# Two batches' scores and attentions back to back, and the transposed weights in the buffer of the weights

## The chip, the core and the metric

The kernel runs on one core of one Trainium2 chip. The metric is device time in microseconds for one launch that computes the whole output. Before the change the median of three runs is 2391.39 us (2390.98 to 2392.63).

A core has a matrix engine (TensorE, PE in the profile, with its weight loads as PEld), VectorE (DVE), ScalarE (ACT), GpSimd (POOL) and SyncE (SP), which here issues nearly all DMAs. Each engine works through its own queue in program order and waits for the others by semaphores. TensorE writes to PSUM, 128 partitions of banks of 512 floats; all other tiles lie in SBUF.

## What is computed

Input `x` has 128 batches of 128 agents with 512 features, in float32, and `adj` one 128x128 adjacency matrix a batch. Two layers follow each other, each with a residual and a layer norm:

```
layer 0:  q, k, v = x Wq + bq, x Wk + bk, x Wv + bv         (8 heads of 64)
          attn    = softmax(where(adj > 0, q k^T / 8, -1e9))  over k, per head
          x1      = layernorm(x + relu(concat(attn v) Wo + bo))
layer 1:  Wh      = x1 W;  s_i = Wh a1;  s_j = Wh a2
          e       = where(adj > 0, leaky(s_i + s_j), -9e15);  att = softmax(e, over i)
          out     = layernorm(x1 + leaky(att Wh))
```

## The kernel before, in words

All products of a weight matrix are done by Strassen's scheme, seven products in place of eight. Q, K and V are made for a group of four batches (`group_product`, tiles `st_y`, `st_w`, `st_x`, L367): 21 pieces a group, 7 for each of Q, K and V, each of 8 TensorE instructions in the profile. The product with `Wo` (`LayerZero`) and with `W1` (`LayerOne`) are made for a pair of batches (`pair_product`, tiles `p_y`, `p_w`, `p_x`, L448): 7 pieces of 4 instructions each.

The softmax of layer 0 for one batch is the class `Softmax`. Its parts are

- `scores`: q k^T of the eight heads, two heads at a time, one on the upper and one on the lower 64 rows of TensorE's array, into two PSUM tiles `lg` (L519, 16 instructions);
- `add` (twice, L533) and `reduce` (L542) on VectorE: mask added while PSUM is read into `pa`, then the maximum of each head; `maxima` is all three;
- `exp` (L553) and `divide` (L567) on ScalarE, one instruction a head, with the sums of `exp` inverted on VectorE by `reciprocals` (L563);
- `store` (L574): `pa`, 512 KB, to DRAM; `fetch` (L580): back as `paz` in four DMAs, with blocks of 32 partitions rearranged; `transpose` (L584): 32x32 blocks turned on VectorE into `paT`. Together they make the transpose of each head's weights;
- `attend` (L597): O^T = V^T attn^T, two heads at a time on the two 64-column halves of the array, into one PSUM tile `p_oT` (16 instructions); `copy` (L611): to SBUF on ScalarE with the bias; `sum`: Strassen's sums of a pair on GpSimd.

Layer 1's attention of one batch is the class `Edge`, with one product `p_h` (L838) of two instructions.

The order of the work is written out by hand: the program switches the scheduler off, and each engine's queue holds its instructions in the order in which Python calls them. The main loop (L981) runs t from -3 to 123. In step t it interleaves a batch's softmax with `group()` (the next group piece), `pair()` (the next pair piece, `LayerZero` in odd steps and `LayerOne` in even ones), with the `Edge` of an earlier batch (`edge`, `fin`, `coming`) and with loads. Five group pieces fall on most steps (six on each fourth) and seven pair pieces. The last four batches and what is left over follow in a hand-written list, `PLAN` (L1242), in which `sl` is the softmax left over from the loop.

In the kernel before, step t does the whole softmax of batch t up to the fetch. Its transposition comes in the middle of step t + 1 (`last.transpose()`, L1097) and its attention at that step's end (`last.attend()`, L1146), just ahead of the next step's scores (L1017). At the end of a step the order on TensorE is therefore `p_h`, `p_oT` of the batch before, `lg` of the next batch, then a group piece.

`lg`, `p_oT`, `p_h`, `p_y`, `p_w` and `p_x` take turns in five PSUM banks (`ps_mm`, L98). `pa`, `paz` and `paT` have one buffer each, but in steps 0, 2 and 4 `pa` lies in another tile's place (`first_homes`).

## Time and profile before

| | us |
|---|---|
| median of three runs | 2391.39 |
| profiled execution, its own time | 2393.51 |
| span from first to last instruction | 2391.6 |
| TensorE busy | 2360.3 (99%) |
| VectorE busy | 1825.5 (76%) |
| ScalarE busy | 1515.4 (63%) |
| GpSimd busy | 814.6 (34%) |
| `lg` on TensorE, 128 blocks of 16 | 148.7 |
| `p_oT` on TensorE, 126 blocks of 16 (and two in other homes) | 137.9 |

The mean granted clock of TensorE is 0.998 of full speed. Between 200 and 2230 us TensorE is busy 2025.8 of 2030 us. The first 60 us hold 53.2 us of TensorE work and the last 161.6 us 143.5, so nearly all of its idle time lies at the two ends.

In a timeline a row is a run of instructions of one kind on one engine: start in us from the start of the span, length, engine, line, operation, output<-inputs, shapes and the number of instructions, and in brackets the idle time ahead of it with what ended it. TensorE's instructions overlap, so that a row's length runs into the next row: what a block costs is the distance from its start to the next start. For DMAs a row's length is the time of issuing; the landing is told separately.

### The profile page before, as it was taken

What the parts mean: (1) busy time and instruction counts of PE and PEld (TensorE: products, weight loads), DVE (VectorE), ACT (ScalarE), POOL (GpSimd) and SP (SyncE); (2) the same over time, 40 slices, a digit from 0 to 9 for tenths busy, and PEclk for the clock granted to TensorE, in tenths of its full rate; (3) what the DMA queues carried; (4) which work ended last, traced back from release to release, by engine and by line L of the source; (5) the groups of instructions that cost most, each with busy time, mean ns of one, the idle gap of its engine ahead of it and who ended that gap; (6) DMA issues with size and microseconds to landing.
All of it is one profiled execution on the core that took longest, in us unless ns stands there. A gap on an engine that the chain in (4) does not pass through costs nothing.

```text
span 2391.6 us, 44137 instructions
## 1 busy us (share of the span) xinstructions
PE 2360.3 (99%) x13362; PEld 1976.1 (83%) x13362; DVE 1825.5 (76%) x3718; ACT 1515.4 (63%) x5459; POOL 814.6 (34%) x1191
## 2 busy tenths in 40 slices
PE   8999999999999999999999999999999999999997
PEld 7888888888888888888888888888888888888875
DVE  5668777787787777877877877778777777787778
ACT  3656666666666666666666666666656666666675
POOL 1333334332343333333333433333323333333335
PEclk9999999999999999999999999999999999999999
DMA  7655555555555555555555555455555554545543
GB/s 204 183 176 157 158 178 156 175 156 161 170 159 168 179 153 169 164 163 180 156 159 178 161 166 166 155 174 164 160 182 159 155 181 148 185 157 161 166 154 115
DMA packets 435565, 395.31 MB, mean 165 GB/s; under 512 B 108280, under 2 KB 339328, under 8 KB 435328
## 3 DMA queue, kind: packets, MB, share of 16 engines
q1 hardware_dynamic: 435008, 392.23, 53.2%
q8 instruction: 107, 1.75, 0.3%
q14 instruction: 130, 1.06, 0.1%
q10 hardware_dynamic: 320, 0.26, 0.0%
HBM read 248.58 MB, written 143.72 MB: 164 GB/s over the span
## 4 chain that ended last, share of the span: by engine, by line
PE 84%; DVE 4%; DMA 4%; ACT 4%; SPq 2%; issue 2%; POOL 1%; DVEq 0%; POOLq 0%; ACTq 0%
PE st_y L367 24%; PE p_y L448 16%; PE st_w L367 12%; PE p_w L448 8%; PE st_x L367 6%; PE lg L519 5%; PE p_oT L597 5%; PE p_h L838 4%; PE p_x L448 4%; ACT pa L567 1%; DMA x_dram<-x 1%; ACT pa L553 1%; SPq L241 1%; DVE st L641 1%; DMA e_dram<-e 1%
## 5 line engine op out<-in xcount | busy, mean ns | idle before, releaser
L553 ACT ACTIVATE pa<-pa,nmax 128x128 f32<-128x128 f32 x1008 | 392.6, 394 | 8.4 <-DVE nmax L542 8.0
L647 POOL TENSOR_SCALAR ve<-mv 128x1 f32<-128x1 f32 x256 | 70.0, 273 | 840.2 <-DVE mv L643 834.8
L567 ACT ACTIVATE pa<-pa,rs 128x128 f32<-128x128 f32 x1008 | 334.1, 395 | 5.4 <-DVE rs L563 5.3
L276 POOL TENSOR_TENSOR oS<-oT 128x256 f32<-128x256 f32 x63 | 45.8, 728 | 639.2 <-ACT oT L611 639.2
L533 DVE TENSOR_TENSOR pa<-lg,mf 128x512 f32<-128x512 f32 x252 | 161.9, 684 | 95.2 <-PE lg L519 94.2
L459 ACT COPY pr_t<-p_y 128x257 f32<-128x257 f32 (+1 forms) x375 | 137.6, 367 | 131.8 <-PE p_y L448 127.7
L344 ACT COPY st_t<-st_y 128x512 f32<-128x512 f32 x192 | 110.5, 576 | 145.7 <-PE st_y L367 144.3
L553 ACT ACTIVATION_READ_ACCUMULATOR pa<-pa,nmax 128x1 f32 x1008 | 192.6, 191 | 0.0
L597 PEld LDWEIGHTS p_oT<-paT,v 128*64 128x64 f32 x2016 | 107.5, 136 | 93.2 <-PE st_y L367 44.0
L649 POOL TENSOR_TENSOR rstd<-ve,mhalf 128x1 f32<-128x1 f32 x256 | 177.0, 691 | 21.3
L611 ACT ACTIVATE oT<-p_oT,b_cols 128x128 f32<-128x128 f32 x504 | 144.2, 369 | 56.8 <-PE p_oT L597 55.8
L348 ACT ACTIVATE st_t<-st_y,b_cols 128x256 f32<-128x256 f32 x192 | 80.6, 471 | 155.3 <-PE st_y L367 155.3
L584 DVE STREAM_TRANSPOSE paT<-paz 128x1024 f32<-128x1024 f32 x126 | 156.9, 1245 | 8.2 <-DMA paz<-pa_dram 7.8
L542 DVE TENSOR_REDUCE nmax<-pa 128x8 f32<-128x1024 f32 x126 | 153.7, 1220 | 4.4
L519 PE MATMUL lg<-kT,qT 64*128 64x128 f32 x2048 | 148.7, 285 | 0.0
L519 PEld LDWEIGHTS lg<-kT,qT 64*128 64x128 f32 x2048 | 124.2, 187 | 22.9 <-issue 22.6
L597 PE MATMUL p_oT<-paT,v 128*64 128x128 f32 x2016 | 137.9, 279 | 1.5 <-DVE paT L584 1.0
L448 PE MATMUL p_y<-wo,oT 128*128 128x256 f32 x504 | 129.7, 380 | 1.9 <-ACT pr_t L459 1.7
L769 DVE TENSOR_TENSOR wh<-p_w,pr_t 128x257 f32<-128x257 f32 x122 | 51.9, 425 | 104.2 <-PE p_w L448 64.1
L448 PE MATMUL p_y<-w,x1T 128*128 128x257 f32 x496 | 128.3, 381 | 2.7 <-ACT wk L459 2.5
L448 PE MATMUL p_y<-wo,oS 128*128 128x256 f32 x504 | 129.6, 379 | 1.1 <-ACT pr_t L459 1.0
L448 PE MATMUL p_y<-w,x1S 128*128 128x257 f32 x496 | 128.1, 380 | 0.2 <-ACT wk L459 0.2
(201 smaller groups left out, 6024.2 us busy)
## 6 DMA issues: line engine op xcount, KB each, us to landing
pa_dram<-pa SPq DMA_DIRECT2D x126, 512.0 KB, 3.2
paz<-pa_dram SPq DMA_DIRECT2D x504, 128.0 KB, 2.8
wv_n<-wv SPq DMA_DIRECT2D x224, 256.0 KB, 2.8
x<-in_x_dram SPq DMA_DIRECT2D x128, 256.0 KB, 3.0
x_dram<-x SPq DMA_DIRECT2D x128, 256.0 KB, 2.6
xz<-x_dram SPq DMA_DIRECT2D x512, 64.0 KB, 2.0
xz<-in_x_dram SPq DMA_DIRECT2D x496, 64.0 KB, 2.3
out_dram<-z SPq DMA_DIRECT2D x120, 256.0 KB, 2.5
```

The costliest lines, as they stand in the source:

```text
L367: nc.tensor.matmul(p[:, m, :], lhs, rhs, start=start and m == 0 and kc == 0, stop=True, skip_group_check=True,)
L448: nc.tensor.matmul(p[:, :width], xs()[n][:, kc, :], w[:, PLACE[n], kc, :], start=start and kc == 0, stop=True, skip_group_check=True,)
L459: nc.scalar.copy(t[:, :width], p[:, :width])
L519: nc.tensor.matmul(self.lg[r][:, c, :], q[rows, c, cols], k[rows, c, cols], start=c == 0, stop=True, skip_group_check=True,)
L533: nc.vector.tensor_add(by_head[:, r * NC : (r + 1) * NC], self.lg[r].rearrange("p c (b k) -> p c b k", b=4), mf.unsqueeze(1).to_broadcast( ...
L542: nc.vector.tensor_reduce(self.nmax, by_head, AX.XY, ALU.max, negate=True)
L553: nc.scalar.activation(self.pa[:, :, h, :], self.pa[:, :, h, :], AF.Exp, bias=self.nmax[:, h : h + 1], accum_out=self.sums[:, h : h + 1],)
L567: nc.scalar.activation(self.pa[:, :, h, :], self.pa[:, :, h, :], AF.Copy, scale=self.rs[:, h : h + 1])
L584: nc.vector.transpose(self.paT.rearrange("p h (a i) -> p a h i", i=32), self.paz.rearrange("p a (h k) -> p a h k", k=32),)
L597: nc.tensor.matmul(self.oT[r * HD : (r + 1) * HD, c, :], v[:, h * HD : (h + 1) * HD], self.paT[:, r * NC + c, :], start=c == 0, stop=True, ...
L611: nc.scalar.activation(OT[pair][:, c, h * P : (h + 1) * P], self.oT[:, c, :], AF.Identity, bias=b_cols[:, 1, c : c + 1],)
L649: nc.gpsimd.tensor_tensor(self.r, ve, mhalf, ALU.pow)
```

## The change

The loop now handles two batches in two steps. In an even step t it makes the scores of batch t (`first`) and of batch t + 1 (`sm`) one behind the other, does the whole softmax of `first` up to the fetch, and of `sm` the adds, the reduction and the first four exponentials (at the end of the step). In the odd step it does the other four exponentials of `sm`, its divisions, its store and its fetch; it transposes `first` in the middle of the step and `sm` near the end; and then both attentions follow each other, then both copies, and the sums of the pair. The next even step begins with two scores again. So at the end of an odd step TensorE has `p_h`, `p_oT`, `p_oT`, `lg` x2 batches, and at the end of an even step `p_h` and then a group piece.

`transpose` writes into `pa` itself, which the store has emptied, viewed as [partition, head, query]; the tile `paT` is gone and `pa` has two buffers. Masks are loaded, cast and scaled two steps ahead instead of one. In `PLAN` the jobs of `sl` and `m1` go, since the loop now ends with all its batches attended. Setup tiles that borrowed the places of `pa`, `paz` and `paT` borrow the two of `pa`.

The diff, cut to its core (an odd step after the first few has the parts under `else`):

```diff
@@ class Softmax
         def tile(self, name, shape):
             home = self.homes and self.homes.get(name)
-            return home(shape) if home else work.tile(shape, F32, name=name)
+            bufs = 2 if name == "pa" else 1
+            return home(shape) if home else work.tile(shape, F32, name=name, bufs=bufs)
...
         def transpose(self):
-            self.paT = self.tile("paT", [P, H, P])
+            flat = self.pa.rearrange("p b h k -> p (b h k)")
+            self.paT = flat.rearrange("p (h q) -> p h q", h=H)
             nc.vector.transpose(
...
@@ main loop
-        if on(t + 1):
-            load_mask(t + 1)
+        if on(t + 2):
+            load_mask(t + 2)
...
-        last, sm = sm, Softmax(t, first_homes if t in (0, 2, 4) else None) if on(t) else none
-        sm.scores()
+        if t % 2 == 0:
+            first, sm = (Softmax(t), Softmax(t + 1)) if on(t) else (none, none)
+            first.scores()
+            sm.scores()
         coming.turn_blocks()
...
         else:
-            sm.maxima()
+            if t % 2 == 0:
+                first.maxima()
             group()
+            if t % 2 == 0:
+                sm.add(0)
+                sm.add(1)
...
             pair()
-            sm.exp(0, 1, 2, 3)
+            if t % 2 == 0:
+                first.exp(0, 1, 2, 3)
+            else:
+                sm.exp(4, 5)
             edge.exp()
             pair()
-            sm.exp(4, 5)
-            last.transpose()
+            if t % 2 == 0:
+                first.exp(4, 5)
+                sm.reduce()
+            else:
+                sm.exp(6, 7)
+                first.transpose()
             group()
-            sm.reciprocals(0)
+            (first if t % 2 == 0 else sm).reciprocals(0)
             pair()
-            sm.exp(6)
+            if t % 2 == 0:
+                first.exp(6)
+            else:
+                sm.reciprocals(1)
             fin.apply()
             fin.store()
-            sm.exp(7)
+            if t % 2 == 0:
+                first.exp(7)
+            else:
+                sm.divide(0, 1)
             edge.divide()
             pair()
-            sm.reciprocals(1)
-            sm.divide(0, 1, 2, 3)
+            if t % 2 == 0:
+                first.reciprocals(1)
+                first.divide(0, 1, 2, 3)
+            else:
+                sm.divide(2, 3, 4, 5)
             coming = Edge(t - 6) if on(t - 6) and t + 1 < END else none
             coming.sender()
             coming.store_sender()
...
             group()
-            sm.divide(4, 5)
+            if t % 2 == 0:
+                first.divide(4, 5)
+            else:
+                sm.divide(6, 7)
             pair()
-            sm.divide(6, 7)
-            if on(t + 1):
-                mask_float(t + 1)
+            if t % 2 == 0:
+                first.divide(6, 7)
+            if on(t + 2):
+                mask_float(t + 2)
             group()
-        sm.store()
+        (first if t % 2 == 0 else sm).store()
...
-        sm.fetch()
+        (first if t % 2 == 0 else sm).fetch()
...
+        if t % 2 == 0:
+            sm.exp(0, 1)
         pair(2)
+        if t % 2 == 0:
+            sm.exp(2, 3)
         if t % 2 == 0 and on(t - 6):
             turn_x1(t)
         if t not in (0, 4):
             group(21 if t % GROUP == 0 else 1)
+        if t % 2 == 1:
+            sm.transpose()
         fin = edge
         fin.product()
         fin.copy()
-
-        last.attend()
-        last.copy()
-        if t % 2 == 0:
-            last.sum(0, 1, 2, 3)
+        if t % 2 == 1:
+            first.attend()
+            sm.attend()
+            first.copy()
+            sm.copy()
+            sm.sum(0, 1, 2, 3)
```

Steps 0 to 4 have the same moves in their own branches, and `PLAN` loses the entries that begin with `sl.` and `m1.`.

More of the change, by code (lines that the diff above doesn't have):

```diff
@@ L175, in load_wv @@
         tiles = [big.tile([P, 2, 2, HALF], F32, name="wv_t", tag="v", bufs=3) for _ in range(3)]
-        tiles.append(work.tile([P, 2, 2, HALF], F32, name="wv_t", tag="paT"))
+        tiles.append(work.tile([P, 2, 2, HALF], F32, name="wv_t", tag="pa", bufs=2))
         t = [tiles[n // 2][:, n % 2] for n in range(7)]
@@ L897 @@
     chores = []
-    sm = fin = edge = coming = none
+    first = sm = fin = edge = coming = none
     def x_turns(t):
@@ L903, in x_turns @@
         return [b for b in [(), (t + 7, t + 8), (t + 8,), (t + 8,)][t % GROUP] if on(b)]
-    x_rows = [work.tile([P, 2, D], F32, name="x_rows", tag=tag) for tag in ("pa", "paz")]
+    x_rows = [work.tile([P, 2, D], F32, name="x_rows", tag="pa", bufs=2) for _ in range(2)]
     for b in range(2):
@@ L978 @@
     END = B - GROUP
-    first_homes = {"pa": lambda shape: work.tile(shape, F32, name="pa", tag="x1T")}
     for t in range(-3, END):
@@ L1025 @@
             group(2)
-        if t < 3:
-            sm.maxima()
+        if t < 3 and t % 2 == 0:
+            first.maxima()
+            sm.add(0)
+            sm.add(1)
             group(2)
@@ L1032 @@
                 sum_x(1)()
-            sm.exp(0, 1, 2, 3)
+            first.exp(0, 1, 2, 3)
             group()
+            first.reciprocals(0)
+            first.exp(4, 5, 6, 7)
+            first.reciprocals(1)
+            sm.reduce()
+            first.divide(0, 1, 2, 3)
+            group()
+            first.divide(4, 5, 6, 7)
+            mask_float(t + 2)
+        elif t < 3:
+            group(2)
+            if on(t - 2):
+                load_residual(t - 2)
+            sm.exp(4, 5)
+            group()
+            sm.exp(6, 7)
             sm.reciprocals(0)
-            sm.exp(4, 5, 6, 7)
+            sm.reciprocals(1)
             if t == 1:
                 group()
-            sm.reciprocals(1)
             sm.divide(0, 1, 2, 3)
-            last.transpose()
+            first.transpose()
             group()
@@ L1045 @@
                 group()
-            if on(t + 1):
-                mask_float(t + 1)
+            if on(t + 2):
+                mask_float(t + 2)
         elif t == 4:
             layer = later.pop()
-            sm.maxima()
+            first.maxima()
             group()
             layer.apply(0)
+            sm.add(0)
+            sm.add(1)
             load_residual(2)
@@ L1056 @@
                 sum_x(2)()
-            sm.exp(0, 1)
+            first.exp(0, 1)
             group()
-            sm.exp(2, 3, 4, 5)
-            last.transpose()
+            first.exp(2, 3, 4, 5)
+            sm.reduce()
             group()
@@ L1066 @@
             w1_chores(3)
-            sm.exp(6, 7)
+            first.exp(6, 7)
             group()
-            sm.reciprocals(0)
-            sm.reciprocals(1)
-            sm.divide(0, 1, 2, 3, 4, 5, 6, 7)
-            mask_float(5)
-        else:
-            sm.maxima()
+            first.reciprocals(0)
+            first.reciprocals(1)
+            first.divide(0, 1, 2, 3, 4, 5, 6, 7)
+            mask_float(6)
+        else:
+            if t % 2 == 0:
+                first.maxima()
             group()
+            if t % 2 == 0:
+                sm.add(0)
+                sm.add(1)
             if t == 3:
@@ L1092 @@
             pair()
-            sm.exp(0, 1, 2, 3)
+            if t % 2 == 0:
+                first.exp(0, 1, 2, 3)
+            else:
+                sm.exp(4, 5)
             edge.exp()
             pair()
-            sm.exp(4, 5)
-            last.transpose()
+            if t % 2 == 0:
+                first.exp(4, 5)
+                sm.reduce()
+            else:
+                sm.exp(6, 7)
+                first.transpose()
             group()
-            sm.reciprocals(0)
+            (first if t % 2 == 0 else sm).reciprocals(0)
             pair()
-            sm.exp(6)
+            if t % 2 == 0:
+                first.exp(6)
+            else:
+                sm.reciprocals(1)
             fin.apply()
             fin.store()
-            sm.exp(7)
+            if t % 2 == 0:
+                first.exp(7)
+            else:
+                sm.divide(0, 1)
             edge.divide()
             pair()
-            sm.reciprocals(1)
-            sm.divide(0, 1, 2, 3)
+            if t % 2 == 0:
+                first.reciprocals(1)
+                first.divide(0, 1, 2, 3)
+            else:
+                sm.divide(2, 3, 4, 5)
             coming = Edge(t - 6) if on(t - 6) and t + 1 < END else none
@@ L1117 @@
             group()
-            sm.divide(4, 5)
+            if t % 2 == 0:
+                first.divide(4, 5)
+            else:
+                sm.divide(6, 7)
             pair()
-            sm.divide(6, 7)
-            if on(t + 1):
-                mask_float(t + 1)
+            if t % 2 == 0:
+                first.divide(6, 7)
+            if on(t + 2):
+                mask_float(t + 2)
             group()
-        sm.store()
+        (first if t % 2 == 0 else sm).store()
         if 0 <= t < 3:
@@ L1134 @@
             load_x(b)
-        if on(t + 1):
-            mask(t + 1)
+        if on(t + 2):
+            mask(t + 2)
+        if t % 2 == 0:
+            sm.exp(0, 1)
         pair(2)
+        if t % 2 == 0:
+            sm.exp(2, 3)
         if t % 2 == 0 and on(t - 6):
@@ L1210 @@
         {"oT": spare("kT", 3)},
-        {"pa": spare("xT", 2), "paz": spare("xS", 2), "paT": spare("qT", 4)},
+        {"pa": spare("xT", 2), "paz": spare("xS", 2)},
         {},
-        {"pa": spare("xT", 2), "paz": spare("xS", 2), "paT": spare("qT", 4)},
+        {"pa": spare("xT", 2), "paz": spare("xS", 2)},
     ]
     fin.on_scalar = True
-    jobs = {"sl": sm, "el": fin, "v": Pieces(v_pieces)}
+    jobs = {"el": fin, "v": Pieces(v_pieces)}
     jobs["v"].fetch = fetch_v
@@ L1242 @@
     PLAN = """
-        el.residual v.p6 x0.x m2.adj m1.adj al.apply.0 x1.x e0.sender sl.transpose s0.scores
-        al.store.0 v.t2 al.fetch.1 v.p5 el.stats m2.cast s0.add.0 m1.cast el.rstd m3.adj s0.add.1
-        s1.scores al.fetch.0 s0.reduce el.apply b0.p1 m2.mask s0.exp.4.5 el.store m1.mask
-        s2.scores s1.add.0 v.fetch s0.exp.6.7 v.fetch s1.add.1 b0.p2 s0.exp.2.3 s1.reduce
-        sl.attend s0.exp.0.1 al.transpose.0 v.p2 s1.exp.6.7 al.transpose.1 s1.exp.2.3
-        s0.reciprocals.0 al.sum.0 s0.reciprocals.1 s0.divide.0.1 v.p7 al.sum.1 v.c11 v.fetch
-        s0.divide.6.7 al.sum.2 s0.divide.2.3 al.sum.3 b1.p1 s0.divide.4.5 v.t3 s0.store b0.t0
-        v.p4 v.c22 s1.exp.0.1 b0.c11 s1.exp.4.5 s1.reciprocals.0 v.p3 s1.divide.0.1 s2.add.0
-        s0.fetch s1.divide.2.3 s2.add.1 v.c21 s2.reduce b0.p6 e1.sender m3.cast b1.p5 sl.copy
-        m3.mask v.c12 s1.reciprocals.1 s2.exp.0.1 b1.p2 sl.sum.0 s0.transpose b0.t2 sl.sum.1
-        s1.divide.4.5 b0.p7 sl.sum.2 s1.divide.6.7 sl.sum.3 s2.exp.6.7 s1.store s2.exp.2.3 b0.t3
+        el.residual v.p6 x0.x m2.adj al.apply.0 x1.x e0.sender s0.scores al.store.0 v.t2
+        al.fetch.1 v.p5 el.stats m2.cast s0.add.0 el.rstd m3.adj s0.add.1 s1.scores al.fetch.0
+        s0.reduce el.apply b0.p1 m2.mask s0.exp.4.5 el.store s2.scores s1.add.0 v.fetch
+        s0.exp.6.7 v.fetch s1.add.1 b0.p2 s0.exp.2.3 s1.reduce s0.exp.0.1 al.transpose.0 v.p2
+        s1.exp.6.7 al.transpose.1 s1.exp.2.3 s0.reciprocals.0 al.sum.0 s0.reciprocals.1
+        s0.divide.0.1 v.p7 al.sum.1 v.c11 v.fetch s0.divide.6.7 al.sum.2 s0.divide.2.3 al.sum.3
+        b1.p1 s0.divide.4.5 v.t3 s0.store b0.t0 v.p4 v.c22 s1.exp.0.1 b0.c11 s1.exp.4.5
+        s1.reciprocals.0 v.p3 s1.divide.0.1 s2.add.0 s0.fetch s1.divide.2.3 s2.add.1 v.c21
+        s2.reduce b0.p6 e1.sender m3.cast b1.p5 m3.mask v.c12 s1.reciprocals.1 s2.exp.0.1 b1.p2
+        s0.transpose b0.t2 s1.divide.4.5 b0.p7 s1.divide.6.7 s2.exp.6.7 s1.store s2.exp.2.3 b0.t3
         s2.reciprocals.0 s2.exp.4.5 b0.p4 s2.divide.0.1 s1.fetch s2.reciprocals.1 b0.c21
```

## Prediction

> **What bounds the kernel now.** First the page's busy line, its chain, and the waits of TensorE's queue, longest first:

> ```profile
> PE 2360.3 (99%) x13362; PEld 1976.1 (83%) x13362; DVE 1825.5 (76%) x3718; ACT 1515.4 (63%) x5459; POOL 814.6 (34%) x1191
> PE 84%; DVE 4%; DMA 4%; ACT 4%; SPq 2%; issue 2%; POOL 1%; DVEq 0%; POOLq 0%; ACTq 0%
> PE p_h L838 <- DVE wk L833: 5.0, 5, 2.6
> PE p_y L448 <- ACT pr_t L459: 3.4, 7, 0.7
> ```

> TensorE is busy 99% of the span, and its longest sum of waits is 5.0 us. Only two things can move the time by a per cent: fewer TensorE microseconds, or a wait put into a queue that has none. The timeline of TensorE through one border between steps (start, length, operation) shows the first:

> ```profile
> 1003.03 1.02 PE L838 MATMUL p_h<-wh,att 128*128 128x512 f32 x2
> 1003.98 1.09 PE L597 MATMUL p_oT<-paT,v 128*64 128x128 f32 x16
> 1005.00 1.16 PE L519 MATMUL lg<-kT,qT 64*128 64x128 f32 x16
> 1006.10 1.99 PE L367 MATMUL st_y<-xT,wk 128*128 128x256 f32 x8
> 1007.93 1.03 PE L448 MATMUL p_y<-w,x1T 128*128 128x257 f32 x4
> ...
> 1009.66 1.89 PE L367 MATMUL st_y<-xT,wq 128*128 128x256 f32 x8
> 1011.39 1.03 PE L448 MATMUL p_y<-w,x1S 128*128 128x257 f32 x4
> ```

> Start to start, a Strassen product of eight instructions takes 1.73 us in ordinary running (1009.66 to 1011.39) but 1.83 behind the scores. p_h takes 0.95 here against 0.86 in the chain. p_oT (64 columns) takes 1.02 and the scores (64 rows) 1.10. What these two cost without their borders is read from two windows that cut a block in the middle:

> ```profile
> 1003.98 0.44 PE L597 MATMUL p_oT<-paT,v 128*64 128x128 f32 x4
> 1040.74 0.94 PE L519 MATMUL lg<-kT,qT 64*128 64x128 f32 x12
> ```

> p_oT: the twelve instructions after the first four take 1.09 - 0.44 = 0.65, so 0.108 per two and 0.87 for sixteen. Scores: the last four take 1.16 - 0.94 = 0.22, so 0.11 per two and 0.89 for sixteen.

> The second thing is how soon a batch's weights can be back on chip. One odd step, TensorE, ScalarE and SyncE:

> ```profile
> 1032.72 1.03 PE L448 MATMUL p_y<-wo,oS 128*128 128x256 f32 x4
> 1033.35 0.57 ACT L344 COPY st_t<-st_y 128x512 f32<-128x512 f32 x1
> 1033.82 0.69 ACT L567 ACTIVATE pa<-pa,rs 128x128 f32<-128x128 f32 x2
> 1034.67 0.70 ACT L567 ACTIVATE pa<-pa,rs 128x128 f32<-128x128 f32 x2
> 1035.39 0.32 SPq L574 DMA_DIRECT2D pa_dram<-pa  x1
> 1038.16 2.52 SPq L580 DMA_DIRECT2D paz<-pa_dram  x4
> 1038.76 1.02 PE L838 MATMUL p_h<-wh,att 128*128 128x512 f32 x2
> ```

> The last division ends at 1035.37, the store goes out at once, the fetch follows 2.77 us later when it has landed, and its four issues take 2.52. p_h, with attention right behind it, starts at 1038.76. Today that attention is of the batch before, so the trip has a whole step, 17.9 us, of cover.

> **The change, part by part.**

> *Fewer borders.* For each pair of batches one border of each kind goes: p_oT 1.02 - 0.87 = 0.15, scores 1.10 - 0.89 = 0.21, the product behind 0.10, p_h in the even step 0.09. That is 0.55 us a pair, all on TensorE, which is the path. The loop has 62 pairs: -34 us. The order of TensorE's instructions in the changed kernel shows 16 `p_oT` and 16 `lg` back to back, so the change does take place.

> *A round trip inside one step.* The second batch of a pair (`sm`) is now divided, stored, fetched, transposed and attended all in the odd step. Its last divisions stand on ScalarE behind the copy of that step's third group product, which waits for TensorE; so the trip cannot start early however idle ScalarE is. Ahead of that copy ScalarE has four exponentials less (1.55, from 1027.14 to 1028.69 for four) and two divisions more (0.6), some 0.95 less, so it reaches the copy before TensorE is done and waits for it. Two forms of odd step:

> (t % 4 = 3) Product done 1032.72; hand-over 0.20 (1007.93 to the copy at 1008.13); copy 0.47; two divisions 0.69: 1034.08, against 1035.37 before. Trip: issue to fetch 2.77 here and 2.65 a pair later (1072.67 to 1075.32), say 2.7; three issues ahead of the last, 1.3 to 1.9, say 1.6; landing of the last 2.8 (median of its DMA row); with hand-overs 0.2, 7.3. Landed 1041.4. The 128x1024 transposition takes 1.25 and the hand-over 0.1: 1042.7. TensorE comes to the second p_oT at 1038.76 + 0.95 + 0.92 (0.87 and a third of its border) = 1040.63. **Stall 2.1 us.**

> (t % 4 = 1) Product done 1070.18; hand-over 0.20; two half copies 0.73; divisions 0.69: 1071.8. Plus 7.3 and 1.35: 1080.45. TensorE: p_h at 1076.22, plus 1.87: 1078.09. **Stall 2.35 us.**

> Mean 2.25 a pair. Steps t = 3 to 123 are 61 pairs: +137 us. Nothing makes it shrink from pair to pair: the trip hangs on a TensorE product 7.9 us ahead of the attention, whenever that comes.

> Bounds of the trip: fastest landings and shortest issues of its rows (2.6 + 3 x 0.30 + 2.3 + 0.05) give 5.85, a stall of 0.8; the latest landing of any odd step in this trace gives 9.5, a stall of 4.45. I take 7.3 because both steps shown lie within 0.5 of it.

> [...]

> *Who is behind the new wait.* On VectorE the transposition waits for the landing; behind it stand `e_turned` (0.3), the x1 apply (0.55) and the next adds. They would be ready at 1042.6 + 0.85 = 1043.5, and the next scores are complete only at 1042.7 + 1.02 + 0.89 + 0.2 = 1044.8, so nothing more is late. On SyncE the fetch waits for the store as before, with the same loads behind it. On ScalarE the copies of p_oT start later with TensorE.

> *Moved work at no price.* Four exponentials (1.55) go to the end of the even step, where ScalarE idles 1.34 and 2.22 us (before L767 and L344). The even step gains two adds and a reduction on VectorE (1.29 + 1.22) and loses a transposition (1.25); it idled 0.66, 0.68, 1.84 and 2.21 there. Mask loads and casts come one step earlier, same number. The second scores need the PSUM bank of the first p_oT of the pair; ScalarE empties it in 1.14 after it ends, and TensorE comes 1.02 + 0.89 later. If that cover were gone it would cost 1.2 a pair; it isn't, and the stall widens it. The missing `paT` tile costs nothing: its place is `pa`, whose exponentials were stored before.

> *Start and end.* At t = 1 the last division ends near 61.2 in both (it follows a copy that waits for TensorE), store 62.68, four weight loads, last fetch issue 67.3, landed 70.1, transposed 71.5; TensorE is ready near 63.0: 8.5, less the 0.77 that it waits there now. +8 us. In the tail the jobs of `sl` leave the plan and one p_oT moves ahead of it: under 1 us either way, taken as 0.

> **Sum.** 2391.6 (span; its execution took 2393.5, the median run 2391.4, so span and median are one number here) - 34 + 137 + 8 = 2502.6. I say **2503 us**, 4.7% slower.

> **The rivals.**

> *Hidden trip: faster.* If the weights were back before TensorE asks, only -34 stays: 2358. It takes a trip of at most 5.2 us in the first form (from 1034.08 to 1040.63, less 1.35) and 4.95 in the second; the pair breaks even where the stall is 0.55, at a mean trip of 5.6. For it: the attention is the last thing in the step. Against: the fastest landings on the rows make 5.85. Chance 4%; level 1%.

> *Half hidden.* A trip of 5.85 to 6.3, the queues being calmer when TensorE runs 5% slower: stalls of 0.8 to 1.25, 2414 to 2442. For it: the DMA share is 0.54, not full. Against: the median landings, 3.2 and 2.8, lie only 0.6 and 0.5 above the fastest, so there is little queueing to lose. 8%.

> *Later still.* A trip over 8.3, or a second wait beside it (the first batch's transposition in the odd step also has only some 9 us from its divisions, and delays the second's divisions when late): over 2564, up to 2391.6 - 34 + 8 + 61 x 4.45 = 2637. 9%. A stall can also cost TensorE's clock: the granted clock stands at 1.00 in the first 60 us in spite of an idle of 1.8 us there.

> [...]

> *Forecast*, a trip of 6.3 to 8.3: stalls 1.25 to 3.25, 2442 to 2564. 78%.

> **How the numbers follow.** The time is that of the forecast. Its own range leaves 22% outside; I widen it by a few us on each side to 2438 and 2570. Faster by over 0.2% (4.8 us, about what a measurement can tell) 4%, within it 1%, slower 95%.

> **What would show it.** Right: TensorE's waits led by p_oT for VectorE's transposition, some 62 times, 2 to 2.5 us each and near 140 in total, between the two attentions; blocks of 32 `p_oT` and 32 `lg`; VectorE waiting for `paz`; PE's busy time down by about 34; the loop's pair of steps at some 37.5 us instead of 35.8. Wrong: p_oT waiting for nothing (hidden trip), or `lg` waiting for ScalarE's copies (banks). The step I trust least is the 7.3 us.

## The result, and the profile after

The changed kernel takes **2647.15 us** (median of four runs, 2639.35 to 2649.59) against 2391.33 (2390.98 to 2392.63) for the kernel before: 1.106 times as long, 95% interval 1.104 to 1.109. The forecast of 2503 had the sign and missed the size: the range ended at 2570.

The profiled execution after has a span of 2647.7 us; before it was 2391.6, so 256.1 us have to be found. First the page of the changed kernel, its busy line and the shares of its chain:

```profile
PE 2440.0 (92%) x13362; PEld 2069.0 (78%) x13362; DVE 1810.6 (68%) x3718; ACT 1515.2 (57%) x5459; POOL 796.9 (30%) x1191
PE 59%; DMA 15%; DVE 10%; ACT 7%; SPq 5%; issue 3%; POOL 1%; DVEq 0%; POOLq 0%; ACTq 0%
```

Two things are to be read here. TensorE's share fell from 99% to 92%, and in the chain DMA, VectorE, ScalarE and SyncE's queue (SPq) have 15, 10, 7 and 5% where they had 4, 4, 4 and 2: there is a wait now. But TensorE is also busy for 79.7 us longer, with the same 13362 instructions. A wait doesn't do that. Something made the instructions themselves longer.

The wait is the longest of TensorE's list of waits (us in total, times, longest):

```profile
PE p_oT L600 <- DVE pa L587: 176.9, 62, 7.1
```

The longer instructions are found in the groups by line and tile (count, then busy us and mean ns of one, then idle us before them):

```profile
L520 PE MATMUL lg<-kT,qT 64*128 64x128 f32 x2048 | 204.9, 377 | 0.0
L600 PE MATMUL p_oT<-pa,v 128*64 128x128 f32 x2016 | 160.2, 309 | 177.3 <-DVE pa L587 176.9 <-DVE rt L835 0.4
```

Before, the scores took 148.7 us in all and p_oT 137.9, in twice as many blocks. Fewer borders should have made both shorter. TensorE's timeline through one border of each form of odd step shows what happened. First t % 4 = 3:

```profile
1081.07 1.09 PE L600 MATMUL p_oT<-pa,v 128*64 128x128 f32 x16
1085.55 1.09 PE L600 MATMUL p_oT<-pa,v 128*64 128x128 f32 x16 [3.38 <-DVE pa L587]
1086.57 3.69 PE L520 MATMUL lg<-kT,qT 64*128 64x128 f32 x32
...
1123.22 1.09 PE L600 MATMUL p_oT<-pa,v 128*64 128x128 f32 x16
1126.49 1.09 PE L600 MATMUL p_oT<-pa,v 128*64 128x128 f32 x16 [2.18 <-DVE pa L587]
1127.51 3.69 PE L520 MATMUL lg<-kT,qT 64*128 64x128 f32 x32
```

The last three lines are the next odd step, t % 4 = 1. The two attentions stand together and the scores are one block of 32, as forecast; between the attentions is the stall, 3.38 and 2.18 us. The new thing is the length of the scores behind it: 3.69 us for 32 instructions, where 16 had taken 1.16 before. The trace's clock records give the reason: in 58 stretches, nearly all 3.413 or 6.827 us long and 238.8 us together, the clock was granted at half, nearly always from within 1.6 us of the end of such a stall. The mean clock of the run is 0.955. (The kernel before has one such stretch, of 13.0 us, at its very end.)

VectorE's timeline in the same two steps completes the picture. In the first the transposition waits for the data:

```profile
1081.57 0.52 DVE L665 TENSOR_SCALAR x<-x,mv,rstd 128x512 f32<-128x512 f32 x1
1084.24 1.25 DVE L587 STREAM_TRANSPOSE pa<-paz 128x1024 f32<-128x1024 f32 x1 [2.16 <-DMA paz<-pa_dram]
...
1124.17 0.51 DVE L665 TENSOR_SCALAR x<-x,mv,rstd 128x512 f32<-128x512 f32 x1
1124.60 0.68 DVE L385 TENSOR_TENSOR qT<-st_w,st_t 128x512 f32<-128x512 f32 x1
1125.20 1.23 DVE L587 STREAM_TRANSPOSE pa<-paz 128x1024 f32<-128x1024 f32 x1
```

In the second (last three lines) it waits for nothing: VectorE comes to it straight from a Strassen sum, the data having landed. So there the stall is not the trip's but the order of VectorE's own queue, in which the last group's sums and normalization stand ahead of the transposition.

The balance: +177 for the stall, some -33 for the borders (below), +107 for scores and p_oT at half clock (204.9 and 160.2 here, less 132.1 and 125.8, which is what the same blocks take in the last version below, which has no stalls). That makes 251 of 256 us.

### The profile page after: what moved, and what is told of

The parts are those of the page before. It is cut to its first block, busy times and chain, and to the rows that moved or that the text cites. A ratio compares the mean times of both kernels' runs of the same rounds, so it can differ in the third digit from the quotient of the medians.

```text
span 2647.7 us, 44071 instructions
## 1 busy us (share of the span) xinstructions
PE 2440.0 (92%) x13362; PEld 2069.0 (78%) x13362; DVE 1810.6 (68%) x3718; ACT 1515.2 (57%) x5459; POOL 796.9 (30%) x1191
## 4 chain that ended last, share of the span: by engine, by line
PE 59%; DMA 15%; DVE 10%; ACT 7%; SPq 5%; issue 3%; POOL 1%; DVEq 0%; POOLq 0%; ACTq 0%
PE st_y L367 16%; PE st_w L367 10%; PE p_y L448 10%; PE lg L520 7%; DMA pa_dram<-pa 7%; DMA paz<-pa_dram 6%; PE p_w L448 5%; DVE pa L587 4%; ACT pa L568 4%; PE st_x L367 4%; SPq L581 4%; PE p_oT L600 3%; PE p_x L448 3%; PE p_h L841 2%; DMA xz<-in_x_dram 1%
## 5 line engine op out<-in xcount | busy, mean ns | idle before, releaser
L568 ACT ACTIVATE pa<-pa,rs 128x128 f32<-128x128 f32 x1008 | 327.2, 393 | 26.5 <-DVE rs L564 26.2
L600 PE MATMUL p_oT<-pa,v 128*64 128x128 f32 x2016 | 160.2, 309 | 177.3 <-DVE pa L587 176.9
L600 PEld LDWEIGHTS p_oT<-pa,v 128*64 128x64 f32 x2016 | 124.4, 152 | 238.5 <-DVE pa L587 191.8
L534 DVE TENSOR_TENSOR pa<-lg,mf 128x512 f32<-128x512 f32 x252 | 161.7, 683 | 170.2 <-PE lg L520 170.2
L459 ACT COPY pr_t<-p_y 128x257 f32<-128x257 f32 (+1 forms) x375 | 138.1, 368 | 203.3 <-PE p_y L448 201.2
L344 ACT COPY st_t<-st_y 128x512 f32<-128x512 f32 x192 | 110.3, 574 | 192.8 <-PE st_y L367 192.5
L587 DVE STREAM_TRANSPOSE pa<-paz 128x1024 f32<-128x1024 f32 x126 | 156.7, 1244 | 80.3 <-DMA paz<-pa_dram 79.3
L520 PE MATMUL lg<-kT,qT 64*128 64x128 f32 x2048 | 204.9, 377 | 0.0
L520 PEld LDWEIGHTS lg<-kT,qT 64*128 64x128 f32 x2048 | 189.7, 282 | 17.5 <-issue 17.1
L543 DVE TENSOR_REDUCE nmax<-pa 128x8 f32<-128x1024 f32 x126 | 151.7, 1204 | 2.3
L448 PE MATMUL p_y<-wo,oT 128*128 128x256 f32 x504 | 129.9, 380 | 4.5 <-ACT p_y L469 3.1
L448 PE MATMUL p_y<-wo,oS 128*128 128x256 f32 x504 | 129.5, 379 | 0.5 <-ACT pr_t L459 0.5
L448 PE MATMUL p_y<-w,x1T 128*128 128x257 f32 x496 | 128.3, 381 | 1.8 <-ACT wk L459 1.8
L448 PE MATMUL p_y<-w,x1S 128*128 128x257 f32 x496 | 128.0, 380 | 0.2 <-ACT wk L459 0.2
L367 PE MATMUL st_y<-xT,wk 128*128 128x256 f32 x512 | 126.3, 390 | 0.0
```

The lines of the kernel that those rows point to most:

```text
L367: nc.tensor.matmul(p[:, m, :], lhs, rhs, start=start and m == 0 and kc == 0, stop=True, skip_group_check=True,)
L448: nc.tensor.matmul(p[:, :width], xs()[n][:, kc, :], w[:, PLACE[n], kc, :], start=start and kc == 0, stop=True, skip_group_check=True,)
L459: nc.scalar.copy(t[:, :width], p[:, :width])
L520: nc.tensor.matmul(self.lg[r][:, c, :], q[rows, c, cols], k[rows, c, cols], start=c == 0, stop=True, skip_group_check=True,)
L534: nc.vector.tensor_add(by_head[:, r * NC : (r + 1) * NC], self.lg[r].rearrange("p c (b k) -> p c b k", b=4), mf.unsqueeze(1).to_broadcast( ...
L543: nc.vector.tensor_reduce(self.nmax, by_head, AX.XY, ALU.max, negate=True)
```

## The experiments

Each kernel starts from the changed one. Where a single time is given it has no interval. Beside them the kernel before took 2389 to 2391 us (medians).

### Keeping TensorE busy in the stall

Five spare products go between the two attentions, on top of all the kernel's own work; they need nothing, and what they write is overwritten by the attention.

```diff
+        def warm(self, n):
+            self.oT = psum("p_oT").rearrange("p (c q) -> p c q", c=NC)
+            for _ in range(n):
+                nc.tensor.matmul(
+                    self.oT[:, 0:2, :],
+                    wk[:, 0, 0, :P],
+                    wk[:, 0, 0, :],
...
             first.attend()
+            sm.warm(5)
             sm.attend()
```

> The changed kernel with five spare 128x256 products of a constant block, put on TensorE between the two attentions, into the bank that the second attention then overwrites; the output stays the same. They fill 10 x 0.216 = 2.2 us of a wait of 2.2 to 3.8 us. Theory A (the idle wait lets TensorE's granted clock fall to 0.5, and the scores behind it pay): the wait's time stays, the clock comes back above 0.99, the block of two scores takes 1.99 in place of 3.35 us, and the time falls by 90 to 120 us to 2530 to 2560. Theory B (the slow scores come from having two batches' scores next to each other, by banks or weight loads): scores stay at 3.3 us and the time at 2640 to 2665.

Measured 2552.49 us (2551.24 to 2553.75), 1.068 times the kernel before (1.066 to 1.070). More work, and 95 us less time; the mean clock is 0.995. TensorE's waits and its timeline (the spare products are the ten instructions of L595):

```profile
PE p_oT L613 <- DVE pa L587: 29.9, 38, 4.7
```

```profile
1000.98 1.09 PE L613 MATMUL p_oT<-pa,v 128*64 128x128 f32 x16
1002.01 2.42 PE L595 MATMUL p_oT<-wk 128*128 128x256 f32 x10
1005.02 1.09 PE L613 MATMUL p_oT<-pa,v 128*64 128x128 f32 x16 [0.59 <-DVE pa L587]
1006.04 2.06 PE L520 MATMUL lg<-kT,qT 64*128 64x128 f32 x32
```

2.42 of the 3 us are filled, the second attention starts hardly sooner (on average 3.84 us after the first, against 3.89), and the scores take 2.06 instead of 3.69. The half clock is down from 238.8 us to 25.4, all of it at the start and the end of the run. This shows that the clock is lost through the idle time: nothing else was taken away. What is left above the kernel before, some 160 us, is the stall itself, filled (150.4 us of spare products) or not (29.9), less the borders.

### How long an idle time costs the clock

Two spare products instead of five, which leave about 1 us less idle in each stall.

> The changed kernel with two spare products between the two attentions in place of five: some 0.95 us of each idle stretch is filled, so that the stalls of 2.17 become about 1.2 and those of 2.5 to 3.8 become about 1.6 to 2.9. The stall and its filling together stay at 177 us. If the half clock follows an idle of about 1.9 us inside one stretch of 3.41, only the longer half of the stalls can set it off, and of those some two in three: 20 or so of half-clock stretches, 25 to 40 us lost in place of 114, in all 2560 to 2590. If only an idle of 3.4 us or more does, none is left, as with five: 2545 to 2555. If any idle over 1 us does, nearly all stay: 2630 to 2650.

Measured 2576.73 us; half clock in 20 stretches, 87.2 us. Two borders of it:

```profile
1015.91 1.13 PE L595 MATMUL p_oT<-wk 128*128 128x256 f32 x4
1018.15 1.09 PE L613 MATMUL p_oT<-pa,v 128*64 128x128 f32 x16 [1.11 <-DVE pa L587]
1019.17 2.06 PE L520 MATMUL lg<-kT,qT 64*128 64x128 f32 x32
...
812.83 1.13 PE L595 MATMUL p_oT<-wk 128*128 128x256 f32 x4
815.99 1.09 PE L613 MATMUL p_oT<-pa,v 128*64 128x128 f32 x16 [2.02 <-DVE pa L587]
817.01 3.60 PE L520 MATMUL lg<-kT,qT 64*128 64x128 f32 x32
```

```profile
842.51 1.09 PE L600 MATMUL p_oT<-pa,v 128*64 128x128 f32 x16 [3.17 <-DVE pa L587]
843.53 2.06 PE L520 MATMUL lg<-kT,qT 64*128 64x128 f32 x32
```

### The trip taken away

The second batch's weights are neither stored nor fetched; its transposition reads the first batch's fetched weights. So the softmax weights of the odd batches are left out of the computation, and with them half of the store and fetch traffic.

```diff
-        (first if t % 2 == 0 else sm).store()
+        if t % 2 == 0:
+            first.store()
...
-        (first if t % 2 == 0 else sm).fetch()
+        if t % 2 == 0:
+            first.fetch()
...
         if t % 2 == 1:
+            sm.paz = getattr(first, "paz", None)
             sm.transpose()
```

> The changed kernel without the store and the fetch of every second batch; its transposition reads what the first batch's fetch left, so this leaves out half of the round trips. Theory A (the landing of the round trip ends the wait, as predicted): p_oT waits for nothing and the time is 2355 to 2380. Theory B (where t % 4 is 1, VectorE's own queue ends it, with the layer norm and a Strassen add ahead of the transposition): waits of 2.2 us stay in every second pair and 1.1 us in the others, the half clock stays behind the longer ones only, and the time is 2490 to 2530.

Measured 2503.20 us, half clock for 67 us. TensorE's wait:

```profile
PE p_oT L600 <- DVE pa L587: 106.5, 63, 5.1
```

VectorE waits for the landing only at the start any more (6.7 us, against 79.3 in 45 times without the edit), and TensorE still waits 106.5 us for VectorE, 5.1 of it at the start. That much is the order of VectorE's queue: some 1.2 us in each step with t % 4 = 3, and 2.2 in each with t % 4 = 1. The trip decides over the rest only.

### The order alone, the trip alone, and both

The order: the transposition moves two pieces up, ahead of the last group's sums and normalization on VectorE.

```diff
-        pair(2)
+        pair()
+        if t % 2 == 1 and t >= 3:
+            sm.transpose()
+        pair()
```

> The changed kernel with the second batch's transposition ahead of the last pair piece's adds and norm on VectorE, the round trip as it was. If VectorE's queue alone made the wait: near 2360. If the trip alone: within 10 us of 2647. If the two are nearly level where t % 4 is 1 (landing 6.9 us after the last division, VectorE 7.3): that wait falls from 2.2 to 1.6 to 1.9 us, the other stays near 3.2, and the time is 2600 to 2640.

Measured 2631.18 us. The stall hardly shrinks, and VectorE now waits three times as long for the landing (79.3 us before the edit), with everything behind the transposition waiting too. A second wait comes with it, of p_y in the even step (2.4 us before the edit):

```profile
PE p_oT L600 <- DVE pa L587: 167.3, 63, 8.1
PE p_y L448 <- ACT pr_t L459: 14.4, 24, 1.2
```

```profile
DVE pa L587 <- DMA paz<-pa_dram: 234.3, 66, 5.6
```

The trip: the second batch's exponentials, divisions and store go to the front of the odd step, ahead of the third group's copy, so that the fetch goes out some 4 us earlier (against the first attention of the pair). The transposition stays in its old place.

```diff
             if t % 2 == 0:
                 first.maxima()
+            else:
+                sm.exp(4, 5, 6, 7)
             group()
...
             if t % 2 == 0:
                 first.exp(0, 1, 2, 3)
             else:
-                sm.exp(4, 5)
+                sm.divide(0, 1, 2, 3, 4, 5, 6, 7)
+                sm.store()
...
             coming.store_sender()
+            if t % 2 == 1:
+                sm.fetch()
```

> The round trip of the second batch some 3.5 us earlier, its transposition where the change has it, behind the norm on VectorE. If the trip alone makes the wait: near 2409, as with both moves. If VectorE's queue also makes it: waits of 1.2 us (t % 4 = 3) and 2.2 us (t % 4 = 1), half clock behind the longer ones, and a time like that of e2_no_trip, 2480 to 2530.

Measured 2495.38 us, half clock 59.7 us, and the stall is that of the kernel with no trip at all (106.5), while p_y waits for 1.0 us only:

```profile
PE p_oT L600 <- DVE pa L587: 105.6, 62, 8.0
```

Both edits together:

> The transposition placed as in e3_place, and in odd steps all exponentials of the second batch at the start, its eight divisions behind the first pair piece, and store and fetch right after: the trip starts some 3.5 us earlier. Same operations, same output. Theory (trip and VectorE's order together make the wait, the wait makes the half clock, and the borders saved are real): no wait of p_oT over 0.5 us, clock above 0.99, and 2391 less 34 for the borders, plus some 10 at the start: 2355 to 2375. If the borders saved nothing: 2390 to 2405. If another wait takes over: above 2410.

Measured 2409.20 us (2406.56 to 2414.28), 1.008 times the kernel before (1.006 to 1.010). TensorE's longest waits:

```profile
PE p_y L448 <- ACT pr_t L459: 17.5, 24, 1.2
PE p_oT L600 <- DVE pa L587: 13.7, 5, 8.1
```

The stall is gone but for the start of the run. Neither edit alone did it: the second attention starts at the later of two times, the landing and VectorE's arrival at the transposition. In the changed kernel the landing comes some 2 us after VectorE with t % 4 = 3, and about 0.4 us ahead of it (median) with t % 4 = 1. Whoever moves one finds the other. But the time is not the 2355 to 2375 expected: a third wait is left, 17.5 us of p_y in the even step. It comes with the new place of the transposition and not with the stall's going: that edit alone had it at 14.4 us beside a stall of 167.3, and the early trip alone had not.

### What is left after that

Four kernels went after the remainder. The first, from the one with both edits, moves the second batch's mask adds in the even step behind the edge layer's statistics:

```diff
             group()
-            if t % 2 == 0:
-                sm.add(0)
-                sm.add(1)
...
             fin.rstd()
+            if t % 2 == 0:
+                sm.add(0)
+                sm.add(1)
```

> e5_both with the second batch's two adds behind the layer-1 maxima and statistics on VectorE instead of ahead of them. In e5_both ScalarE waits 63 us in total for those maxima, and the pair piece p4 of even steps then waits for ScalarE's copy (st_y ahead of it takes 2.08 in place of 1.73 us each fourth step, a loss of some 33 us). Theory: the waits go and the time is 2370 to 2385, faster than before the change. If the PSUM banks of the second scores now hold up a later product, or another copy is late: 2400 or above.

Measured 2408.09 us (2403.63 to 2411.38), 1.008 times before (1.006 to 1.009); TensorE's wait for ScalarE's copy (p_y for pr_t) went up, from 17.5 to 23.3 us. The move gained nothing; 2370 to 2385 had been expected.

The second, on top of it, takes away the wait at the start: batches 1 and 3 are transposed and attended one step later, with the weights of batches 0 and 3 in the free x1T place meanwhile.

```diff
+            late = sm if t in (2, 4) else none
+            if on(t):
+                first = Softmax(t, early_home if t == 0 else None)
+                sm = Softmax(t + 1, early_home if t == 2 else None)
...
-        if t % 2 == 1:
+        if t in (2, 4):
+            late.attend()
+            late.copy()
+            late.sum(0, 1, 2, 3)
+        if t in (1, 3):
+            first.attend()
+            first.copy()
+        if t % 2 == 1 and t >= 5:
```

> e6_adds with batches 1 and 3 attended one step later, as before the change, their weights in the place of a tile not yet in use. In e5_both the start holds waits of 8.1 and 3.5 us and 17 us at half clock, worth some 17 us. Theory: those go, and the time is 12 to 18 us below e6_adds, 2355 to 2370.

Measured 2398.65 us (2395.93 to 2401.04), 1.004 times before (1.002 to 1.005): 9.4 us less, where 12 to 18 had been expected. The stall of p_oT is down to 2.8 us in the whole run; the wait of p_y in the even step is up to 29.8.

The third moves all of the second batch's maximum (two adds and a reduction) to the middle of the even step:

```diff
-            if t % 2 == 0:
-                sm.add(0)
-                sm.add(1)
...
-                sm.reduce()
...
             coming.store_sender()
             if t % 2 == 0:
+                sm.maxima()
```

> e7_start with the second batch's adds and reduction of even steps moved behind the edge sender, to VectorE's idle time. In e7_start p4 of each second even step still waits 0.4 to 1.35 us (29.8 us in all) for a ScalarE copy that stands behind the edge sender, which waits for VectorE's c11 add, which stands behind those adds. Theory: these waits fall below 5 us and the time is 2365 to 2378, faster than before by some 0.7%. If the second batch's exponentials at the end of the even step are now late and hold a later copy: 2385 or above.

Measured 2400.29 us (2398.60 to 2409.63), 1.005 times before (1.004 to 1.006), where 2365 to 2378 had been expected. p_y's wait is gone, and p_w has one:

```profile
PE p_w L448 <- DVE wh L772: 24.5, 29, 1.1
```

VectorE's timeline there, with the adds and the reduction (L534, L543) ahead of the sum `wh` that TensorE waits for, and TensorE's:

```profile
1055.63 1.49 DVE L665 TENSOR_SCALAR z<-z,mv,rstd 128x512 f32<-128x512 f32 x1 [0.93 <-POOL rstd L652]
...
1057.23 1.10 DVE L836 TENSOR_SCALAR att<-att,rt 128x128 f32<-128x128 f32 x1
...
1058.67 1.25 DVE L534 TENSOR_TENSOR pa<-lg,mf 128x512 f32<-128x512 f32 x2
1059.96 1.22 DVE L543 TENSOR_REDUCE nmax<-pa 128x8 f32<-128x1024 f32 x1
1061.10 0.68 DVE L385 TENSOR_TENSOR v<-st_x,st_t 128x512 f32<-128x512 f32 x1
1061.69 0.42 DVE L772 TENSOR_TENSOR wh<-p_w,pr_t 128x257 f32<-128x257 f32 x1
```

```profile
1062.26 1.11 PE L448 MATMUL p_w<-w,x1T 128*128 128x257 f32 x4 [1.12 <-DVE wh L772]
```

`p_w` may be written again only when `wh` has read it. So the 2.5 us were to go behind that sum. The fourth does that:

```diff
-            if t % 2 == 0:
-                sm.maxima()
-            else:
+            if t % 2 == 1:
                 sm.fetch()
...
             pair()
             if t % 2 == 0:
                 first.divide(6, 7)
+                sm.maxima()
...
-        if t % 2 == 0:
+        if t in (0, 2, 4):
             sm.exp(0, 1)
         pair()
         if t % 2 == 1 and t >= 5:
             sm.transpose()
+        if t % 2 == 0 and t >= 6:
+            sm.exp(0, 1)
         pair()
```

> What is different from e8_late_adds: in the even step the second batch's adds and its maximum move behind the last pair of pieces, and its first two exponentials one piece later. Theory (nothing is left but VectorE's order in the even step): in e8_late_adds TensorE's product p3 of every second even step waits for VectorE's add c22, which stands behind the 2.5 us of the second batch's maximum; between the products 200 and 2000 us these starts cost 26 us over the 25 steps, about 33 in the whole run. With the maximum behind c22 that wait goes, and nothing on TensorE waits for it before the next step: 2400 - 33 = 2367 us, 2362 to 2380, so faster than the kernel before by about 1%, with TensorE's waits of p_w and p_y under 8 us together. Rival (the even step has no free place on VectorE for these 2.5 us at all): the wait turns up at a third place, p_h or the next p_oT or a Strassen product behind a late copy, with 20 to 35 us, and the time stays at 2390 to 2405.

Measured **2365.49 us** (2364.81 to 2367.18), 0.990 times the kernel before (0.988 to 0.992): 1% less than the kernel before, and 282 us less than the changed one. Its page's busy line, TensorE's wait for the transposition and one border:

```profile
PE 2329.4 (99%) x13362; PEld 1976.7 (84%) x13362; DVE 1850.5 (78%) x3718; ACT 1509.3 (64%) x5459; POOL 766.6 (32%) x1191
```

```profile
PE p_oT L600 <- DVE pa L587: 4.3, 3, 2.6
```

```profile
1029.94 2.33 PE L600 MATMUL p_oT<-pa,v 128*64 128x128 f32 x32
1032.20 2.06 PE L520 MATMUL lg<-kT,qT 64*128 64x128 f32 x32
```

VectorE now has the sum `wh` first and the maximum right behind it:

```profile
1045.68 0.43 DVE L772 TENSOR_TENSOR wh<-p_w,pr_t 128x257 f32<-128x257 f32 x1 [0.65 <-ACT pr_t L459]
1046.02 1.28 DVE L534 TENSOR_TENSOR pa<-lg,mf 128x512 f32<-128x512 f32 x2
1047.33 1.22 DVE L543 TENSOR_REDUCE nmax<-pa 128x8 f32<-128x1024 f32 x1
```

The two attentions and the two scores run back to back with no stall, and TensorE's busy time is 30.9 us under the 2360.3 of before. This is what the change could give, with its trip out of the way.

## Why the prediction was wrong, step by step

**Fewer borders, 0.55 us a pair, -34: right.** In the last kernel, means from start to start between 200 and 2000 us: p_oT 1.916 a pair against 2 x 1.024 before (0.13 less; the term had 0.15), scores 1.985 against 2 x 1.092 (0.20; it had 0.21), p_h 0.905 against 0.952 in both steps (0.09; it had 0.09), and the product behind the scores no longer there in the even step, 1.73 against 1.83 (0.10; it had 0.10). Together 0.53, over 62 pairs 33 us.

**The stall, 2.25 us a pair, +137: right in kind, too small, and half of its reason missing.** It measured 176.9 us with 7.1 at the start, so 2.78 a pair. By form: t % 4 = 3 was given 2.1 and has 3.13 on average; t % 4 = 1 was given 2.35 and has 2.43, but largely for another reason.

- In the first form the trip, from the end of the last division to the landing, has a median of 7.8 us where 7.3 was taken. And ScalarE was not waiting for TensorE at the third group's copy, as the step said. The copy starts 0.71 after the product is done (1074.07), not 0.20, since two lots of work stand ahead of it:

```profile
1072.71 1.86 ACT L568 ACTIVATE pa<-pa,rs 128x128 f32<-128x128 f32 x6 [0.66 <-DVE rs L564]
1074.48 0.39 ACT L798 ACTIVATE e<-mf,wh 128x128 f32<-128x128 bf16 x1
1074.78 0.56 ACT L344 COPY st_t<-st_y 128x512 f32<-128x512 f32 x1
```

  The divisions had themselves waited 0.66 for VectorE's reciprocals. The longer trip and the later copy, 0.5 each, are most of the 1.03 that was missing.
- In the second form the trip has a median of 7.0, a little under 7.3. In 17 of 30 such steps the stall is 2.17 or 2.18, the same number to 0.01, with VectorE waiting for nothing. The step looked for who is queued behind the transposition and never for what is queued ahead of it. The two experiments with the trip away or early show this floor as some 100 us of stall past the start.

**The clock, which had no term in the sum: the step that failed.** The sum has nothing for TensorE's clock. The reason taken from the profile was that the clock stood at 1.00 in spite of an idle time of 1.8 us in the first 60, and the clock was named only beside the longer stalls of a rival. In the changed kernel all but 7 of the stalls past the start were followed by half clock, at 107 us in scores and p_oT alone, and with five spare products in each stall the run took 95 us less. TensorE's busy time, which was to fall by 34, rose by 79.7. The 1.8 us was read too far: by an estimate that carries the grid back from the one half-clock stretch of that trace, the grid cuts it into 1.59 and 0.23, less than the 1.84 of the shortest that half clock followed in the changed kernel. And the profile did show what a longer stall does: the trace of the kernel before has an idle time of 2.62 near its end, 2.44 of it inside one grid stretch, and the clock stands at 0.50 from 2380.74 on:

```profile
2379.77 1.15 PE L838 MATMUL p_h<-wh,wk 128*128 128x512 f32 x2 [2.62 <-DVE wk L833]
2381.58 2.04 PE L838 MATMUL p_h<-wh,wk 128*128 128x512 f32 x2 [0.66 <-DVE wk L833]
```

The second of these products, of the same form, takes 2.04 in place of 1.15. The term belonged in the sum with a bound on each side: nothing, and, with the stretch that the changed kernel then showed, half of 3.413 for each pair. With the 107 measured the forecast would have been 2610, and 33 of the 37 us that are left are the stall's 0.53 a pair.

**VectorE waiting for `paz`**, as a sign of being right, held in all 31 steps with t % 4 = 3 but in 10 of the 31 with t % 4 = 1 (68.7 us; VectorE's 45 waits and 79.3 us for landings hold four of other transpositions). In the other 21 something else limits the time.

**Moved work at no price: right for the changed kernel.** There no wait of TensorE besides p_oT's is above 4.3 us in all. It no longer held once the second batch's transposition had moved up on VectorE: then the same batch's maximum, which had been said to fit in VectorE's idle times, stood ahead of what TensorE waits for, 17.5 to 29.8 us in three different places of the even step, until it stood behind the sum `wh`. VectorE had the time for it, but not at every place.

**Start, +8: right for the stall** (7.1 us), plus a stretch of 10.2 us at half clock around it that was not counted.

**The rivals.** The hidden trip could not be had by the change as it was made. The version with the trip and the order mended comes to 2365.5 where that rival had 2358. The "later still" rival named stalls up to 4.45 and gave them up to 2637; the mean was 2.78, which on its own lies in the range of the forecast: 2391.6 - 34 + 177 = 2535. What carried the time out of the range is the clock.

## What to carry to other kernels

When a change puts a wait on an engine that was never idle, price two things beside the wait: the clock that it may cost after each idle time (here 107 us in scores and p_oT), and what stands ahead of the releasing instruction on the releaser's own queue. Where a wait has two limits (here the landing and VectorE's order), removing one shows only the distance to the other: the order alone took 16 us off, the trip alone 152, both together 238. Move both, and look at what waits next. And a busy time that grows with the same number of instructions is not made by waiting (here TensorE's 13362 instructions took 79.7 us longer, and it was the clock): look for it in the groups before looking at the waits.

## What the runs showed of the hardware that was not expected

- In the changed kernel, past the start, a half-clock stretch followed 54 of 61 stalls: those with 1.84 to 3.29 us of idle inside one stretch of the 3.413 us grid, and none of the 7 with 1.50 to 1.78. Work that nobody needs was cheaper here than the idle time: ten spare instructions, 2.42 us together, in each pair of steps made the run 95 us shorter.
- In the timeline shown of the third of the last four kernels VectorE's scale of a 128x512 tile took 1.49 us (1055.63) and the one of 128x128 1.10 (1057.23). GpSimd's Strassen sums ran beside both:

```profile
1055.56 1.28 POOL L276 TENSOR_TENSOR xS<-xT 128x512 f32<-128x512 f32 x1
1056.92 1.33 POOL L277 TENSOR_TENSOR xS<-xS,xT 128x512 f32<-128x512 f32 x1
```

  In the next even step of that kernel, with GpSimd idle at that point, the same two took 0.55 and 0.28. Over its whole trace the 29 scales of 128x128 that had such GpSimd sums beside them for over nine tenths of their time took 1.10 to 1.11, and the other 99 at most 0.57. The traces of the kernels before and after have the same two groups, 29 at 1.10 to 1.11 and 99 at 0.28 to 0.57; but 29 of the 99 had such sums beside them for 0.85 or 0.86 of their time and took 0.56 or 0.57. No kernel was run with these sums moved, so that GpSimd is the cause was not tested.
